# A batch of 64x64 matrix exponentials: from one 64-partition half to both halves of the partitions

## The chip, the cores and the metric

The kernel runs on one core of a Trainium2 chip. Time is device time in microseconds (us) of one execution of the program on that core. The core's engines work side by side and are ordered by semaphores: TensorE (PE, matrix products; its weight loads are listed as PEld), VectorE (DVE), ScalarE (ACT), GpSimd (POOL) and SyncE (SP, which here only issues DMAs). The profile is taken from one execution of its own. Its lines name the source line (L1355 is line 1355 of the kernel), the engine, and the tile written and those read.

## The reference

The input `x` has 4 batches of 512 tokens with 288 channels. A transformer block comes first, and then a rotation that depends on the batch:

```python
h = modulate(ln(x)); attn = 16 heads of width 18; x = x + g_msa * proj(attn)
xn = modulate(ln(x)); 4 experts, each token goes to 2 of them
x = x + g_mlp * moe(xn)

U, _ = qr(P)                                   # 288 x 64
v = silu(cond) @ W.T + b                       # 2016 numbers per batch
A = skew-symmetric 64 x 64 matrix made of v    # one per batch
R = expm(A)                                    # 64 x 64, one per batch
z = x @ U
x_out = x + (z @ R - z) @ U.T
```

Everything is float32. The change lies in the path from `v` to `U (R - I)`: four skew matrices of 64x64, one per batch, their exponentials, and the product with `U`.

## The kernel before

The whole work is in `fast_path`; a second path, `general_path`, runs only where a flag at the end says that some bound did not hold. All instructions are issued in an order written out by hand, so each engine takes its instructions in the order of the source as it is executed.

**Stage 1, attention** (about the first 336 us). A loop over `n`, 16 pairs of a batch and a group of four heads, and inside it over `t`, four blocks of 128 keys. Each of these 64 steps issues: `weigh` (four products `z` at L1676, in four groups of 32 rows of the array, and two exponentials `es` at L1685 on ACT), `gather` of the step before (four products `av` at L1694, in four groups of 32 columns), then the pieces that the dictionary `steps` has for this place (projections `pq` L1653, values `pv` L1623, transposes `pt` L1141, the merge `po` L1750, routing, and `column`, one step of a Householder factorisation of `P` on DVE, L1480 to L1523), then one piece from the list `beside`, then one or two `scatter_next`. The two `z` tiles are the only ones, so the `z` of a step waits until the exponentials of the step before have read theirs.

`beside` holds, among others, the two chains that the change touches. `skew_matrices` loads `W`, makes `v` on PE, stores it row by row into a 64x(4x64) matrix `udr` in DRAM (66 DMAs on SP, L1264) that POOL has cleared by a store of zeros (L1236), loads it back as `um` (L1271, SP), and subtracts the transpose: `A = um - um^T` (L1276, L1279). `rotations` returns the pieces of the exponential, and `exponentials` puts an empty piece behind each of them, so that one comes in every second step:

- `norm`: four copies of the identity `I4` (L1315), and a sum of squares per batch (`sqa`, L1321);
- `levels`: their sums over the partitions (`pf`, L1333), six comparisons that say how often each batch's matrix is to be halved (L1338 to L1345), the scaled matrix `pw[0]` (L1346) and its negative `An` (L1349);
- `power(1..3)`: the powers of the matrix, four products `pw` at L1355 and a copy (L1362) each;
- `horner(3..0)`: a polynomial of degree 16 in groups of four, with DVE operations on all four batches at once (L1374, L1376, L1380, L1384) and, but for the first, four products `ph` at L1355;
- `turn`: the transpose `Y` of the result `X` (`pxt`, L1389, and a copy, L1390);
- `square(0..5)`: eight products `psq` (L1395 and L1398: `X X` and its transpose) and two copies under a mask (L1402, L1403);
- `last`: `X - I` (L1406).

All of these tiles have 64 partitions, and 4x64 columns: the batches lie side by side. Every product therefore works with the rows 0 to 63 and the columns 0 to 63 of the array.

`bank` hands out PSUM tiles in turn from a few buffers, so that a product can wait for a copy that reads an earlier tile of another chain.

Routing: when the second batch of a half is merged, DVE computes the slots of its tokens (`slots_of`, L2003) and POOL then sends 16 scatters `slots<-xr` (L2006), one after the other. After them the rows of the first expert are loaded (`xg`, L2050 to L2055), and PE transposes these (`pt`, L2089) at the end of stage 1.

**Stage 2, the experts** (to about 712 us): eight expert passes, `hidden` (`ph`, L2295 and L2308) and `outputs` (`pe`, L2355), one piece of the list `rest` after each tile of work. Among these pieces are the rest of the factorisation, which gives `uT` (`U^T`, held twice, in partitions 0 to 63 and 64 to 127), then `all_fit` (the flag, with `norms`), and `subspace`: `UR = U^T` times `X`, three products `pu` (L2269), each followed by a copy (L2276). `finish` uses `UR` at L2421, `pz`.

**The end** (to 743.7 us): the last four pairs of token tiles are loaded, added, rotated and stored.

Of the kernel before, what the change touches and what calls it, by code (L numbers as in the profile page):

```python
# [10 lines left out]
F32 = mybir.dt.float32  # L11
# [7 lines left out]
P = 128  # L19
# [794 lines left out]
def fast_path(  # L814
# [60 lines left out]
    A = big.tile([D, B, D], F32, name="A")  # L875
# [6 lines left out]
    norms = big.tile([P, B + 1], F32, name="norms")  # L882
    XY = big.tile([D, 2, B, D], F32, name="XY")
# [70 lines left out]
    with ExitStack() as s1:  # L954
# [261 lines left out]
        def skew_matrices(between):  # L1216
# [6 lines left out]
            um = skew.tile([D, B, D], F32, name="um")  # L1223
# [5 lines left out]
            def loads():  # L1229
                for i in range(4):  # L1230
                    nc.gpsimd.dma_start(
                        out=wr[:, :, ts(i, width)],
                        in_=wrT[:, ts(i, width)].rearrange("(k p) f -> p k f", p=CC),
                    )
                nc.gpsimd.memset(um, 0.0)
                nc.gpsimd.dma_start(out=udr, in_=um)  # L1236
                nc.gpsimd.memset(brs, 0.0)
                for i in range(4):
                    nc.gpsimd.dma_start(
                        out=brs[i * HQ : i * HQ + B, :],  # L1240
                        in_=br[ts(i, width)].partition_broadcast(B),
                    )
# [27 lines left out]
            def load():  # L1270
                nc.sync.dma_start(out=um, in_=udr)  # L1271

            def last():
                pt = bank([P, N], "ptA")
                for b in range(B):
                    nc.tensor.transpose(  # L1276
                        pt[:D, ts(b, D)], um[:, b, :], ident[:D, :D]
                    )
# [3 lines left out]
                    pt[:D, : B * D],  # L1282
# [14 lines left out]
        def rotations():  # L1297
# [4 lines left out]
            fs = ep.tile([D, B], F32, name="fs")  # L1302
            need = ep.tile([D, SQUARINGS_FAST, B], F32, name="need")
            shrink = ep.tile([D, B], F32, name="shrink")
            I4 = ep.tile([D, B, D], F32, name="I4")
            pw = ep.tile([D, 4, B, D], F32, name="pw")
            An = ep.tile([D, B, D], F32, name="An")
# [6 lines left out]
            def norm():  # L1314
                nc.vector.tensor_copy(  # L1315
                    I4, ident[:D, :D].unsqueeze(1).to_broadcast([D, B, D])
                )

                for b in range(B):
                    sq = ep.tile([D, C], F32, tag="pr", name=f"sqa{b}")  # L1320
# [10 lines left out]
            def levels():  # L1331
                pf = bank([P, N], "pf")
                nc.tensor.matmul(pf[:D, :B], every[:D, :D], fs, start=True, stop=True)  # L1333
                nc.vector.tensor_copy(norms[:D, :B], pf[:D, :B])

                nc.vector.memset(shrink, 1.0)
                for k in range(SQUARINGS_FAST):
                    nc.vector.tensor_scalar(  # L1338
                        need[:, k, :], norms[:D, :B], THETA2 * 4.0**k, None, ALU.is_gt
                    )  # L1340
                    fk = ep.tile([D, B], F32, tag="fk", name=f"fk{k}")
# [5 lines left out]
                    pw[:, 0], A, shrink.unsqueeze(2).to_broadcast([D, B, D]), ALU.mult  # L1347
                )
                nc.vector.tensor_scalar_mul(An, pw[:, 0], -1.0)  # L1349

            def product(name, lhsT, rhs):
                pa = bank([P, N], name=name)
                pa = pa[:D, : B * D].rearrange("p (b d) -> p b d", b=B)
                for b in range(B):
                    nc.tensor.matmul(  # L1355
                        pa[:, b, :], lhsT[:, b, :], rhs[:, b, :], start=True, stop=True
                    )
# [8 lines left out]
            def horner(i):  # L1366
# [7 lines left out]
                nc.vector.tensor_scalar_mul(m, I4, c[0])  # L1374
# [11 lines left out]
            def turn():  # L1386
                pa = bank([P, N], "pxt")
                for b in range(B):
                    nc.tensor.transpose(pa[:D, ts(b, D)], X[:, b, :], ident[:D, :D])  # L1389
                nc.vector.tensor_copy(flat(Y), pa[:D, : B * D])  # L1390

            def square(k):
                pa = bank([D, 2, B, D], f"psq{k}")
                for b in range(B):
                    nc.tensor.matmul(  # L1395
                        pa[:, 0, b, :], Y[:, b, :], X[:, b, :], start=True, stop=True
                    )
                    nc.tensor.matmul(  # L1398
                        pa[:, 1, b, :], X[:, b, :], Y[:, b, :], start=True, stop=True
                    )  # L1400
                mask = need[:, k, :].bitcast(I32).unsqueeze(2).to_broadcast([D, B, D])
                nc.vector.copy_predicated(X, mask, pa[:, 0])  # L1402
                nc.vector.copy_predicated(Y, mask, pa[:, 1])  # L1403

            def last():
                nc.vector.tensor_sub(X, X, I4)  # L1406
# [11 lines left out]
        def triangular():  # L1418
# [160 lines left out]
            def half():  # L1579
# [4 lines left out]
                    norms[:D, B:], R, AX.X, ALU.max, apply_absolute_value=True  # L1584
                )
                nc.vector.tensor_scalar_mul(norms[:D, B:], norms[:D, B:], 64.0)
# [194 lines left out]
        BH = B // HALVES  # L1781
# [454 lines left out]
    with ExitStack() as s2:  # L2236
# [28 lines left out]
        def subspace():  # L2265

            for k in range(NK):
                pa = bank([P, N], f"pu{k}")
                nc.tensor.matmul(  # L2269
                    pa[:CC, : B * D],  # L2270
                    uT[:D, ts(k, CC)],
                    XY[:, 0].rearrange("p b d -> p (b d)"),
                    start=True,
                    stop=True,
                )
                nc.vector.tensor_copy(  # L2276
                    UR[:, k].rearrange("p b d -> p (b d)"), pa[:CC, : B * D]
# [179 lines left out]
        def all_fit():  # L2457
# [4 lines left out]
            for i, limit in enumerate((1.0e30, 1.0e20)):  # L2462
# [17 lines left out]
            small_ = fin.tile([P, B + 1], F32, name="small_")  # L2480
# [13 lines left out]
                float(P * (2 * B * NG + HALVES * E + B + 1)) - 0.5,  # L2494
# [138 lines left out]
```

## Time and profile before

| what | value |
|---|---|
| median of 3 runs | 745.1 us (744.53 to 746.78) |
| the profiled execution's own time | 745.39 us |
| its span | 743.7 us |
| PE busy | 705.4 us (95%) |
| DVE busy | 503.3 us (68%) |
| ACT busy | 279.9 us (38%) |
| POOL busy | 232.5 us (31%) |
| stretch 120 to 300 us: PE busy | 174.4 of 180 us |
| stretch 120 to 300 us: DVE busy | 144.9 of 180 us |
| products `pw`, `ph` at L1355 | 155.1 to 219.9 us, 48 matmul records |
| products `psq` at L1395 and L1398 | 236.5 to 292.8 us, 96 matmul records |

The span is the time from the first to the last instruction; 1.7 us of the execution lie outside it. A product in float32 appears as two matmul records and two weight loads; a transpose appears as one of each. A form such as `64*96 64x256` gives the rows and columns of the array that are used, and then the moving operand (partitions x columns). The views used below: the timeline of one engine (start, length, engine, line, operation, tiles, form, count, and in brackets the idle time before it with what ended it), the groups of instructions by form (busy time and mean duration in ns), and the chain that ended last, which follows the last instruction back through what released each one.

### The profile page before, as it was taken

What the parts mean: (1) busy time and instruction counts of PE and PEld (TensorE: products, weight loads), DVE (VectorE), ACT (ScalarE), POOL (GpSimd) and SP (SyncE); (2) the same over time, 40 slices, a digit from 0 to 9 for tenths busy, and PEclk for the clock granted to TensorE, in tenths of its full rate; (3) what the DMA queues carried; (4) which work ended last, traced back from release to release, by engine and by line L of the source; (5) the groups of instructions that cost most, each with busy time, mean ns of one, the idle gap of its engine ahead of it and who ended that gap; (6) DMA issues with size and microseconds to landing.
All of it is one profiled execution on the core that took longest, in us unless ns stands there. A gap on an engine that the chain in (4) does not pass through costs nothing.

```text
span 743.7 us, 11406 instructions
## 1 busy us (share of the span) xinstructions
PE 705.4 (95%) x3627; PEld 404.4 (54%) x3627; DVE 503.3 (68%) x2222; ACT 279.9 (38%) x431; POOL 232.5 (31%) x323
## 2 busy tenths in 40 slices
PE   5999999999999999989999999999999999999936
PEld 4432334334343435325677777777677676767723
DVE  3565778796987777885189888988888882013223
ACT  2455554454535444554223323232232323213202
POOL 4035900610035023750154253613123040232331
PEclk9999999999999999999999999999999999999977
DMA  9547700000000001055142543255353240342133
GB/s 227 144 127 205 258 3 6 1 2 2 2 1 2 3 26 59 34 152 136 57 119 66 177 116 121 77 138 168 66 167 72 84 143 18 96 153 73 48 110 128
DMA packets 65493, 66.68 MB, mean 90 GB/s; under 512 B 31608, under 2 KB 55965, under 8 KB 65424
## 3 DMA queue, kind: packets, MB, share of 16 engines
q1 hardware_dynamic: 57040, 41.90, 20.5%
q0 software_dynamic: 7360, 22.91, 9.5%
q10 hardware_dynamic: 1024, 1.07, 0.6%
q8 instruction: 30, 0.49, 0.3%
q14 instruction: 39, 0.32, 0.1%
HBM read 48.08 MB, written 18.09 MB: 89 GB/s over the span
## 4 chain that ended last, share of the span: by engine, by line
PE 67%; DVE 13%; DMA 6%; issue 6%; POOL 4%; ACT 2%; SPq 1%; DVEq 0%; POOLq 0%; ACTq 0%
PE pe L2355 19%; PE ph L2295 18%; PE pq L1653 6%; PE z L1676 4%; PE po L1750 4%; PE ph L2308 3%; PE av L1694 3%; PE pv L1623 2%; DMA rr<-den 2%; PE pt L2089 1%; DVE wj L1487 1%; ACT es L1685 1%; DMA yc<-chosen 1%; DVE q L1476 1%; DMA xg<-slots 1%
## 5 line engine op out<-in xcount | busy, mean ns | idle before, releaser
L2355 PE MATMUL pe<-w2s,hm 128*128 128x288 f32 (+1 forms) x648 | 164.2, 408 | 0.0
L1685 ACT ACTIVATE es<-z 128x1024 f32<-128x1024 f32 x128 | 124.1, 1021 | 83.8 <-PE z L1676 83.8
L2295 PE MATMUL ph<-xgT,w1s 128*128 128x288 f32 (+2 forms) x576 | 152.0, 413 | 0.4
L2355 PEld LDWEIGHTS pe<-w2s,hm 128*128 128x128 f32 (+1 forms) x648 | 118.4, 187 | 31.0 <-issue 2.1
L2295 PEld LDWEIGHTS ph<-xgT,w1s 128*128 128x128 f32 x576 | 105.7, 190 | 40.6 <-issue 11.3
L2317 ACT ACTIVATE hm<-ph,b1r 128x576 f32<-128x576 f32 (+2 forms) x72 | 49.8, 737 | 130.1 <-PE ph L2308 130.1
L1676 PE MATMUL z<-qk 32*128 32x512 f32 x512 | 89.9, 640 | 3.0 <-ACT es L1685 3.0
L1653 PE MATMUL pq<-hT,wqk 96*128 96x512 f32 x192 | 90.5, 608 | 0.0
L2367 POOL TENSOR_TENSOR y<-y,gb 128x288 f32<-128x288 f32 x36 | 29.7, 826 | 144.5 <-ACT y L2366 144.4
L1694 PE MATMUL av<-es,vt 128*32 128x512 f32 x512 | 68.8, 605 | 0.0
L1653 PEld LDWEIGHTS pq<-hT,wqk 96*128 96x128 f32 x192 | 34.3, 191 | 53.9 <-issue 39.2
L2366 ACT ACTIVATE y<-pe,weight 128x288 f32<-128x288 f32 x36 | 18.0, 500 | 118.3 <-PE pe L2355 118.3
L2006 POOL DMA_INDIRECT slots<-xr,where x32 | 32.7, 1021 | 92.4 <-DVE where L2003 48.6
L1676 PEld LDWEIGHTS z<-qk 32*128 32x128 f32 x512 | 25.8, 182 | 48.4 <-ACT es L1685 32.4
L1760 POOL TENSOR_TENSOR xs<-xs,og 128x288 f32<-128x288 f32 x16 | 12.6, 801 | 125.7 <-DVE og L1759 125.7
L1660 ACT ACTIVATE qk<-pq,bqk 128x512 f32<-128x512 f32 x32 | 22.0, 687 | 69.9 <-PE pq L1653 68.1
L1476 DVE SCALAR_TENSOR_TENSOR q<-q 64x1 f32<-64x1 f32 (+1 forms) x192 | 43.5, 226 | 7.0
L2368 POOL DMA_INDIRECT chosen<-y,place x36 | 36.8, 1021 | 19.2 <-DMA chosen<-y,place 10.3
L1487 DVE STREAM_SHUFFLE wj<-pt 32x288 f32<-32x288 f32 (+47 forms) x96 | 42.1, 438 | 0.7
L1694 PEld LDWEIGHTS av<-es,vt 128*32 128x32 f32 x512 | 10.2, 108 | 48.4 <-issue 42.6
L1750 PE MATMUL po<-wp,oT 128*128 128x288 f32 x128 | 33.8, 412 | 1.1 <-DVE oT L1734 0.6
L1475 DVE RECIPROCAL q<-q 64x1 f32<-64x1 f32 (+1 forms) x192 | 30.5, 159 | 4.4
(269 smaller groups left out, 911.6 us busy)
## 6 DMA issues: line engine op xcount, KB each, us to landing
w2s<-in_w_dram SPq DMA_DIRECT2D x8, 1296.0 KB
w1s<-in_w_dram SPq DMA_DIRECT2D x8, 1152.0 KB
slots<-empty POOLq DMA_DIRECT2D x36, 148.0 KB, 2.8
yc<-chosen SPq DMA_DIRECT2D x8, 576.0 KB
out_dram<-xs SPq DMA_DIRECT2D x8, 288.0 KB
wr<-in_wrT_dram POOLq DMA_DIRECT2D x4, 567.0 KB, 8.8
xg<-slots SPq DMA_DIRECT2D x4, 512.0 KB
xg<-slots SPq DMA_DIRECT2D x3, 640.0 KB
```

The source lines that it names most:

```text
L1476: nc.vector.scalar_tensor_tensor(s, u, part, s, ALU.mult, ALU.add)
L1487: nc.vector.stream_shuffle(wj[o : o + HQ, j:], pt[o0 : o0 + HQ, j:], [j % HQ] * HQ)
L1653: nc.tensor.matmul(pq, wqk[:, k, i, ts(g, P)], hT[:, k, :], start=(k == 0), stop=(k == NK - 1),)
L1676: nc.tensor.matmul(zs[c // 2][:, c % 2, :], qk[ts(c, HQ), 1, ts(t, P)], qk[ts(c, HQ), 0, :], start=True, stop=True,)
L1685: nc.scalar.activation(e, z, AF.Exp, scale=SCALE)
L1694: nc.tensor.matmul(avs[n][ts(c, HQ), :], vts[b % 2][:, t, 4 * g + c, :], es[c // 2][:, c % 2, :], start=(t == 0), stop=(t == NT - 1),)
L1750: nc.tensor.matmul(po, oTs[b][:, g, ts(t, P)], wp[:, g, :], start=(g == 0), stop=(g == NG - 1),)
L2006: nc.gpsimd.indirect_dma_start(out=slots[h], out_offset=bass.IndirectOffsetOnAxis(ap=where[:, i, t : t + 1], axis=0), in_=xrs[t // NT][:, ...
L2295: nc.tensor.matmul(ph[:, j, :SB], w1s[:, k, ts(f, P)], xgT[:, k, ts(j, SB)], start=(k == 0), stop=False,)
L2317: nc.scalar.activation(hm[:, f, : CAPS[r]].rearrange("p (j s) -> p j s", j=NB), ph[:, :, :SB], AF.Gelu_apprx_tanh, bias=b1r[:, h, r, f : f ...
L2355: nc.tensor.matmul(po[ts(m, rows), :], slots_[:, f, :], w[:, f, :], start=(f == 0), stop=(f == NF - 1),)
L2368: nc.gpsimd.indirect_dma_start(out=chosen[h], out_offset=bass.IndirectOffsetOnAxis(ap=place[:, t : t + 1], axis=0), in_=y, in_offset=None, ...
```

## The change

Two batches go to partitions 0 to 63 and two to partitions 64 to 127. The tiles `A`, `XY`, `um`, `fs`, `need`, `shrink`, `I2` (was `I4`), `pw`, `An` and `norms` have 128 partitions and half the columns. `each` issues the products of one batch of either half in turn: the products of the first half use the rows 0 to 63 and columns 0 to 63 of the array, those of the second the rows 64 to 127 and columns 64 to 127, and both write one PSUM tile, to partitions 0 to 63 and 64 to 127. The transposes at L1276 and L1389 become products with the identity. The last squaring no longer computes the transpose. The store of zeros and the load of `um` become two DMAs each, and `pf` two products. `subspace` makes two groups of three products, one for each half, with one copy for each group.

```diff
-    A = big.tile([D, B, D], F32, name="A")
+    BH = B // 2
+    A = big.tile([2 * D, BH, D], F32, name="A")
-    norms = big.tile([P, B + 1], F32, name="norms")
-    XY = big.tile([D, 2, B, D], F32, name="XY")
+    norms = big.tile([P, BH + 1], F32, name="norms")
+    XY = big.tile([2 * D, 2, BH, D], F32, name="XY")
...
-                nc.gpsimd.dma_start(out=udr, in_=um)
+                for h in range(2):
+                    nc.gpsimd.dma_start(
+                        out=udr[:, ts(h, BH), :], in_=um[ts(h, D), :, :]
+                    )
...
             def load():
-                nc.sync.dma_start(out=um, in_=udr)
+                for h in range(2):
+                    nc.sync.dma_start(out=um[ts(h, D), :, :], in_=udr[:, ts(h, BH), :])

             def last():
                 pt = bank([P, N], "ptA")
-                for b in range(B):
-                    nc.tensor.transpose(
-                        pt[:D, ts(b, D)], um[:, b, :], ident[:D, :D]
-                    )
+                for b in range(BH):
+                    for h in range(2):
+                        at = ts(h, D)
+                        nc.tensor.matmul(
+                            pt[at, ts(b, D)],
+                            um[at, b, :],
+                            ident[at, at],
+                            start=True,
+                            stop=True,
+                        )
...
             def norm():
-                nc.vector.tensor_copy(
-                    I4, ident[:D, :D].unsqueeze(1).to_broadcast([D, B, D])
-                )
-
-                for b in range(B):
-                    sq = ep.tile([D, C], F32, tag="pr", name=f"sqa{b}")
+                for h in range(2):
+                    at = ts(h, D)
+                    nc.vector.tensor_copy(
+                        I2[at], ident[at, at].unsqueeze(1).to_broadcast([D, BH, D])
+                    )
+
+                for b in range(BH):
+                    sq = ep.tile([P, C], F32, tag="pr", name=f"sqa{b}")
...
-                nc.tensor.matmul(pf[:D, :B], every[:D, :D], fs, start=True, stop=True)
-                nc.vector.tensor_copy(norms[:D, :B], pf[:D, :B])
+                for h in range(2):
+                    at = ts(h, D)
+                    nc.tensor.matmul(
+                        pf[at, :BH], every[at, at], fs[at, :], start=True, stop=True
+                    )
+                nc.vector.tensor_copy(norms[:, :BH], pf[:, :BH])
...
+            def each(out_, lhsT, rhs):
+
+                for b in range(BH):
+                    for h in range(2):
+                        at = ts(h, D)
+                        nc.tensor.matmul(
+                            out_[at, b, :],
+                            lhsT[at, b, :],
+                            rhs[at, b, :],
+                            start=True,
+                            stop=True,
+                        )

             def product(name, lhsT, rhs):
                 pa = bank([P, N], name=name)
-                pa = pa[:D, : B * D].rearrange("p (b d) -> p b d", b=B)
-                for b in range(B):
-                    nc.tensor.matmul(
-                        pa[:, b, :], lhsT[:, b, :], rhs[:, b, :], start=True, stop=True
-                    )
+                pa = pa[:, : BH * D].rearrange("p (b d) -> p b d", b=BH)
+                each(pa, lhsT, rhs)
                 return pa
...
             def turn():
-                pa = bank([P, N], "pxt")
-                for b in range(B):
-                    nc.tensor.transpose(pa[:D, ts(b, D)], X[:, b, :], ident[:D, :D])
-                nc.vector.tensor_copy(flat(Y), pa[:D, : B * D])
+                nc.vector.tensor_copy(Y, product("pxt", X, I2))

             def square(k):
-                pa = bank([D, 2, B, D], f"psq{k}")
-                for b in range(B):
-                    nc.tensor.matmul(
-                        pa[:, 0, b, :], Y[:, b, :], X[:, b, :], start=True, stop=True
-                    )
-                    nc.tensor.matmul(
-                        pa[:, 1, b, :], X[:, b, :], Y[:, b, :], start=True, stop=True
-                    )
-                mask = need[:, k, :].bitcast(I32).unsqueeze(2).to_broadcast([D, B, D])
+                pa = bank([P, 2, BH, D], f"psq{k}")
+                mask = need[:, k, :].bitcast(I32).unsqueeze(2).to_broadcast([P, BH, D])
+                each(pa[:, 0], Y, X)
+                more = k + 1 < SQUARINGS_FAST
+                if more:
+                    each(pa[:, 1], X, Y)
                 nc.vector.copy_predicated(X, mask, pa[:, 0])
-                nc.vector.copy_predicated(Y, mask, pa[:, 1])
+                if more:
+                    nc.vector.copy_predicated(Y, mask, pa[:, 1])
...
         def subspace():
-            for k in range(NK):
-                pa = bank([P, N], f"pu{k}")
-                nc.tensor.matmul(
-                    pa[:CC, : B * D],
-                    uT[:D, ts(k, CC)],
-                    XY[:, 0].rearrange("p b d -> p (b d)"),
-                    start=True,
-                    stop=True,
-                )
+            for h in range(2):
+                pa = bank([P, N], f"pu{h}")
+                pa = pa[:CC, : NK * BH * D].rearrange("p (k n) -> p k n", k=NK)
+                for k in range(NK):
+                    nc.tensor.matmul(
+                        pa[:, k, :],
+                        uT[ts(h, D), ts(k, CC)],
+                        XY[ts(h, D), 0].rearrange("p b d -> p (b d)"),
+                        start=True,
+                        stop=True,
+                    )
                 nc.vector.tensor_copy(
-                    UR[:, k].rearrange("p b d -> p (b d)"), pa[:CC, : B * D]
+                    UR[:, :, ts(h, BH), :].rearrange("p k b d -> p k (b d)"), pa
                 )
```

The remaining lines change the shapes of the small tiles in the same way, and the count that the flag is compared with.

## The prediction

> **What bounds the kernel now.** I read the page's shares first: PE is busy for 95% of the span. The chain that ended last agrees, with 67% PE and 13% DVE.
>
> ```profile
> PE 705.4 (95%) x3627; PEld 404.4 (54%) x3627; DVE 503.3 (68%) x2222; ACT 279.9 (38%) x431; POOL 232.5 (31%) x323
> ...
> PE 67%; DVE 13%; DMA 6%; issue 6%; POOL 4%; ACT 2%; SPq 1%; DVEq 0%; POOLq 0%; ACTq 0%
> ```
>
> What the change touches runs from 137 to 303 us and at 672 us, so the question is whether an instruction saved there moves what follows. PE's timeline of 136 to 345 us shows it:
>
> ```profile
> 155.08 0.68 PE L1355 MATMUL pw<-pw,An 64*64 64x64 f32 x8 [0.79 <-DVE An L1349]
> 155.68 1.14 PE L1676 MATMUL z<-qk 32*128 32x512 f32 x8
> ...
> 161.86 0.64 PE L1141 MATMUL pt<-ident,xh 128*96 128x128 f32 x4 [0.82 <-DVE pw L1362]
> ...
> 210.50 4.15 PE L1750 MATMUL po<-wp,oT 128*128 128x288 f32 x16 [0.51 <-DVE og L1759]
> ...
> 228.08 0.41 PE L1389 MATMUL pxt<-ident,XY 64*64 64x64 f32 x4
> 228.42 1.14 PE L1676 MATMUL z<-qk 32*128 32x512 f32 x8
> ...
> 236.47 0.33 PE L1395 MATMUL psq<-XY 64*64 64x64 f32 x2
> 236.63 0.28 PE L1398 MATMUL psq<-XY 64*64 64x64 f32 x2
> ...
> 237.54 1.14 PE L1676 MATMUL z<-qk 32*128 32x512 f32 x8
> ...
> 332.76 0.63 PE L2089 MATMUL pt<-ident,xg 128*128 128x128 f32 x4 [1.78 <-DMA xg<-slots]
> ```
>
> Read it thus: eight records of `pw` hold PE for 0.60 us before the next `z`, the sixteen of one squaring for 1.07 us, four transposes for 0.34 us. Few gaps lie between; the ones that matter are in brackets, and they name DVE three times and at the end a load. Where a `z` waits for ACT's exponential, that exponential followed the `z` before it, so an earlier start passes through.
>
> The last gap leads to POOL's timeline:
>
> ```profile
> 268.49 1.13 POOL L2006 DMA_INDIRECT slots<-xr,where  x1 [33.53 <-DVE where L2003]
> 271.90 0.98 POOL L2006 DMA_INDIRECT slots<-xr,where  x1 [2.28 <-DMA slots<-xr,where]
> ...
> 302.42 0.30 POOL L1120 TENSOR_SCALAR rs<-mv 128x4 f32<-128x4 f32 x1 [0.60 <-DVE mv L1119]
> ...
> 322.16 0.93 POOL L2050 DMA_DIRECT2D xg<-slots  x1 [2.12 <-DMA slots<-xr,where]
> ```
>
> The scatters start when DVE has `where` (268 us) and pace themselves by their landings, some 2.8 us each, up to the load that PE awaits at 332.76. From there to 712 us PE has no gap worth naming, so what is gained by 332 us is gained at the end.
>
> **PE's price of a product.** Squaring starts a record every 0.057 us (0.28 us for two, the next pair 0.117 us later). Do two quarters run side by side? Two kinds of half do: at `pz` (twelve records, two column halves) two start within 0.03 us, and `z` starts four row groups within 0.03 us.
>
> ```profile
> 685.32 0.88 PE L2421 MATMUL pz<-xT,UR 96*64 96x128 f32 x12
> ```
>
> The twelve records leave PE after 0.81 us. One behind the other, at 128/64 of 0.057 us, they would need 1.37 us. Quarters on the diagonal share neither rows nor columns; no row shows two row groups writing one PSUM tile at once. Bounds: full overlap (half the time) and none (0.057 us each as now), and below that a stop at every switch (rivals). I take full overlap, the nearest rows being `pz` and `z`. Then:
> - a product of four batches, 8 records in pairs, saves 4 x 0.057 = 0.23 us; there are six (`pw`, `ph`);
> - squarings 0 to 4, 16 records: 0.46 us each; the last keeps 8 of 16 records and pairs them: 12 x 0.057 = 0.69 us;
> - the transposes become 8 records, four pairs: about 0 (without overlap +0.23 us each);
> - `pf` has 4 records for 2, at most +0.15 us. PE waits there 0.92 us, until DVE's last `sqa` at 145.9 us; four `sqa` become two, so the cover stays.
>
> The Trainium skill speaks against this: "TensorEngine Tiling (Array Packing)", section "Restrictions and Gotchas", says that different row tiles write different PSUM banks and cannot access the same one simultaneously, and here both halves write one bank. By that rule the pairs take turns and the sum is the no-overlap one below; no run so far shows either.
>
> **DVE's price.** An operation goes by columns, not by partitions: `of` at L1953 with 128x256 takes 0.41 us, as the 64x256 ones at L1376 do. From the two rows below, a column costs (692 - 448) / 224 = 1.09 ns, so 128 fewer save 0.14 us; I take 0.13.
>
> ```profile
> L1734 DVE TENSOR_TENSOR oT<-oraw,rd 128x512 f32<-128x512 f32 x9 | 6.2, 692 | 0.8
> ...
> L1759 DVE TENSOR_TENSOR og<-po,gates 128x288 f32<-128x288 f32 x8 | 3.4, 448 | 4.5 <-PE po L1750 4.5
> ```
>
> Bounds are 0 and 0.2 us (the 64x64 `sqa` takes 0.21). The cheaper kind (L1349, L1374: 0.28 us, and 0.15 at 64x4) saves 0.07 us. The six rounds of small comparisons stay.
>
> **The sum, along the chain.** The chain's view passes between DVE and PE, so I follow the shift of whichever is later.
> 1. To 155 us: POOL's `xh` and `xr` (eight operations, 140.7 to 147.4 us) and DVE's `xh` lead, untouched. `I2` in two parts and `sqa` are under POOL's cover. `pw[0]` saves 0.13, `An` 0.07: shift -0.20.
> 2. 161.86: PE waits 0.82 us for DVE's copy of `pw`, another 0.13 there: -0.33. The first product's saving is lost in that wait.
> 3. `pw` 2 and 3 on PE: -0.79 at 176 us. DVE waits for PE at 181.6 (`vt`) and takes this on.
> 4. 187 to 210: DVE leads. Two `horner` pieces, 0.07 + 4 x 0.13 = 0.59 each: -1.97. PE has -0.79 and two `ph`, -1.25, plus the 0.51 it waits at 210.50: -1.76. The later one holds: -1.76.
> 5. The third `ph`: -1.99. The other DVE savings (two `horner`, `turn`, 11 masked copies for 12) lie beside PE.
> 6. `turn` 0; squarings 0 to 2: -3.37 at 259.7. DVE's `vt` waits for PE at 263.5, and `where` at 268 follows: POOL's scatters start 3.37 earlier.
> 7. Squarings 3 to 5: PE -4.98 at 293 us. POOL's waits of 0.60 at 302.42 and 0.76 at 305.89, for DVE, go; late next is the spacing of the scatter at 304 (2.8 us behind the one at 300.83). POOL: about -4.5 by 306, and so is the load. PE's wait at 332.76 grows by the other 0.5.
> 8. `subspace`: now 1.78 us on PE, in which its third product waits for a copy (0.31 us without a matmul). After: 12 records of 128 columns, 0.114 us each, 1.37 us and about 0.14 to empty: -0.3. The two copies (96x384, about 0.55 us each) end before `pz` at 685 us.
>
> Together -4.8 us: 745.39 - 4.8 = 740.6 against the profiled execution. The median lies 0.3 below it: **740.3 us**, -0.65%.
>
> **DMAs.** POOL issues a second store of zeros, 0.57 us at 57 us; behind it are `brs`, of which the fourth waits 1.48 us for another reason, and which are first read at 78 us. SP issues a second load of `um`, 0.50 us at 126.5; behind it are the four `den` DMAs, which end 2 us before DVE reads them at 134.67, and `um`'s reader is at 136.6. Both cost nothing; without that cover, 0.5 us each.
>
> **Rivals.** *No overlap on PE.* The rule above speaks for it, `pz` and `z` against. Then the chain is -0.33 at 176, -0.84 at 210.5 (the 0.51 of wait, DVE's saving being larger), +0.23 for `turn`, -0.61 at `where`, about -1.1 on POOL, -0.3 at `subspace`: -1.4, 743.7 us. No measurable change; 0.3%, 2.2 us, is what can be told.
>
> *Slower: every switch between halves empties the array.* A lone record lasts 0.218 us against a pitch of 0.057, so a switch costs at most 0.16. A four-batch product has four switches, +0.64 for six; a full squaring eight, +1.28 for five; the last +0.64 - 0.46; `turn` +0.87. Five of the products count: 3.2 + 6.4 + 0.2 + 0.9 = 10.7, less about 1.2 of DVE's and the other savings: +9.5, 754.6 us. With some 72 switches it decides from (1.2 + 2.2) / 72 = 0.05 us each. Against it: the changes of row group in `z` cost nothing that shows.
>
> *Only part arrives.* POOL stays at `where`'s shift and the scatters' spacing gives nothing back: -3.4 - 0.3, 741.4 us. Speaks for it: each scatter but two waits for the one before. On the other side, `sqa` and `I2` out of POOL's way, or full DVE savings of 0.2, could bring -6.5: 738.6.
>
> **How the numbers follow.** Full overlap, in whole or in part: 0.75, from 738.6 to 741.9. No overlap 0.14, around 743.7. A switch that costs: 0.08. The rest, 0.03, is spread. The range to 744.4 takes in most of no overlap and leaves out the slow end: 738.5 to 744.4. Faster by over 0.3% (under 742.9): 0.75 and little of no overlap, 0.76; within: 0.15; slower: 0.09.
>
> **What would show it.** In the changed profile `z` should follow 0.37 us after a `pw` starts (now 0.60) and 0.61 after a squaring (now 1.07); DVE's 128x128 operations should take about 0.28 us; the scatters should start near 265.1 us; `ph` should begin at 338.1 - 4.5 = 333.6. Wrong would be: 0.60 and 1.07 unchanged (no overlap), more (switches), or a gap before 332 that eats the gain.

## The result: the same time, and the profile after

The changed kernel took 747.43 us (median of 20 runs, 744.33 to 749.8), the kernel before, beside it on the same chip, 747.54 us (20 runs, 743.78 to 749.57). The ratio is 1.000, 95% interval 0.9987 to 1.0014: no difference that can be measured. The forecast was 740.3 us against 745.1 us, the median of the first three runs of the kernel before: a ratio of 0.9936. So the 0.65% did not arrive.

The page of the changed kernel hardly differs in its shares: PE lost 1.2 us of busy time, DVE 3.0 us, and the chain that ended last runs 68% through PE.

```profile
PE 704.2 (94%) x3635; PEld 401.7 (54%) x3635; DVE 500.3 (67%) x2217; ACT 280.3 (38%) x431; POOL 231.7 (31%) x324
...
PE 68%; DVE 13%; DMA 6%; issue 5%; POOL 3%; ACT 2%; SPq 1%; DVEq 0%; POOLq 0%; ACTq 0%
```

PE's timeline of the changed kernel, 136 to 345 us, answers to the one shown of before (start, length, engine, line, operation, tiles, form, count, and in brackets the idle time before it and what ended it):

```profile
156.07 0.45 PE L1375 MATMUL pw<-pw,An 64*64 64x64 f32 x8 [0.66 <-DVE An L1368]
156.45 1.14 PE L1700 MATMUL z<-qk 32*128 32x512 f32 x8
...
158.52 0.64 PE L1144 MATMUL pt<-ident,xh 128*96 128x128 f32 x4
162.72 1.09 PE L1144 MATMUL pt<-ident,xh 128*96 128x128 f32 x4 [3.56 <-DVE pw L1391]
163.74 2.09 PE L1700 MATMUL z<-qk 32*128 32x512 f32 x8
165.76 1.94 PE L1718 MATMUL av<-es,vt 128*32 128x512 f32 x8
...
170.27 0.45 PE L1375 MATMUL pw<-pw,An 64*64 64x64 f32 x8
...
240.89 0.68 PE L1375 MATMUL psq<-XY 64*64 64x64 f32 x16
241.50 1.14 PE L1700 MATMUL z<-qk 32*128 32x512 f32 x8
...
293.95 0.45 PE L1375 MATMUL psq<-XY 64*64 64x64 f32 x8
294.33 1.14 PE L1700 MATMUL z<-qk 32*128 32x512 f32 x8
...
334.85 0.63 PE L2112 MATMUL pt<-ident,xg 128*128 128x128 f32 x4 [2.44 <-DMA xg<-slots]
335.41 1.55 PE L1700 MATMUL z<-qk 32*128 32x512 f32 x8
...
341.19 4.04 PE L2320 MATMUL ph<-xgT,w1s 128*128 128x320 f32 x14
```

In the kernel before, the first two groups of transposes stood on PE's timeline in one row:

```profile
157.75 1.08 PE L1141 MATMUL pt<-ident,xh 128*96 128x128 f32 x8
```

Three things are to be seen. First, the products became as short as forecast: `z` follows `pw` after 0.38 us (0.60 before), a full squaring after 0.61 (1.07), the last squaring after 0.38 (1.07). Second, there is a gap that was not there: at 162.72 the second group of transposes `pt` waits 3.56 us for DVE's copy of `pw`. Before, both groups ran in one go at 157.75 us, and only the third waited, 0.82 us, at 161.86. Third, what follows the gap is slow: `z` takes 2.09 us (1.14 behind `pw`, and 1.28 in this place before), `av` 1.94 instead of 1.06. The same happens again, after a shorter wait, at 334.85.

The slowness is the clock. These are windows of the changed kernel (stretch, its length, then the busy time and number of instructions of PE, PEld, DVE, ACT and POOL; the number behind these five is the granted clock of PE, then come the share of the DMA engines and GB/s):

```profile
160.00:162.00 2.00, 0.00 (x0) 0.00 (x0) 2.00 (x11) 0.28 (x1) 0.00 (x0) 0.98 0.04 3
162.00:164.00 2.00, 1.28 (x8) 0.90 (x12) 1.63 (x8) 0.15 (x1) 0.00 (x0) 0.50 0.01 1
164.00:166.00 2.00, 2.00 (x12) 0.46 (x16) 1.76 (x9) 0.70 (x2) 0.00 (x0) 0.50 0.00 0
166.00:168.00 2.00, 2.00 (x10) 0.36 (x3) 0.60 (x5) 2.00 (x3) 0.00 (x0) 0.50 0.00 0
168.00:170.00 2.00, 2.00 (x10) 1.49 (x8) 0.00 (x0) 1.13 (x2) 0.00 (x0) 0.81 0.01 1
```

So from about 162 to 169 us PE ran at half its clock, 0.50 in three windows. In the kernel before, the granted clock was 1.00 in all of these stretches.

DVE's timelines, first of the changed kernel, then of the kernel before, show what PE waited for: the copy is in its old place, behind the sixteen operations `pl` of the routing, of which one starts every 0.38 us.

```profile
162.00 0.46 DVE L1840 SCALAR_TENSOR_TENSOR pl<-xr,wg 128x288 f32<-128x288 f32 x1
...
162.38 0.29 DVE L1391 COPY pw<-pw 128x128 f32<-128x128 f32 x1
```

```profile
161.39 0.41 DVE L1362 COPY pw<-pw 64x256 f32<-64x256 f32 x1
```

So the copy came no later than before, seen from the work around it (9.81 us behind the start of the projection `pq` ahead of it, 9.94 before); another group of transposes now waits for it. In the built programs' lists of semaphores that each instruction waits for, the second group of batch 2 (`k` = 1 in `modulate_T`) waited for ACT before and the third for DVE; now the second waits for DVE and the third for nothing new. In stage 1 the order and number of the calls of `bank` did not change. Every third call there gets a buffer of its own; the others draw on a pool with two buffers under one tag, and the source does not say which of the two a tile gets: that is settled when the program is built. In the changed program the second and the third group have exchanged their buffers, so that the second now takes the buffer that the first `pw` has just used. Two later pairs are exchanged as well, a `pv` with a `pq` and a `psq` with a `pt`.

The executions lie about 1 us apart before the change has an effect, so I compare positions from the start of the projection `pq` just ahead of the first `pw` (151.45 us before, 152.57 after). The second `pw` then comes 5.1 us later than before (17.70 against 12.60 us). From there the gain builds up as planned: the last squaring ends only 0.3 us later than before. Then comes the second fall of the clock, and `ph` begins 2.0 us later in this execution.

### The profile page after: what moved, and what is told of

Read it like the earlier page. It is cut to its first block, busy times and chain, and to the rows that moved or that the text cites. A ratio compares the mean times of both kernels' runs of the same rounds, so it can differ in the third digit from the quotient of the medians.

```text
span 747.4 us, 11416 instructions
## 1 busy us (share of the span) xinstructions
PE 704.2 (94%) x3635; PEld 401.7 (54%) x3635; DVE 500.3 (67%) x2217; ACT 280.3 (38%) x431; POOL 231.7 (31%) x324
## 3 DMA queue, kind: packets, MB, share of 16 engines
q10 hardware_dynamic: 1024, 1.07, 0.6%
## 4 chain that ended last, share of the span: by engine, by line
PE 68%; DVE 13%; DMA 6%; issue 5%; POOL 3%; ACT 2%; SPq 1%; DVEq 0%; POOLq 0%; ACTq 0%
PE pe L2380 19%; PE ph L2320 18%; PE pq L1677 6%; PE z L1700 6%; PE po L1774 4%; PE ph L2333 3%; PE av L1718 3%; PE pv L1647 2%; DMA rr<-den 2%; DMA yc<-chosen 2%; ACT es L1709 1%; PE pt L2112 1%; DVE wj L1511 1%; DVE q L1500 1%; DMA xg<-slots 1%
## 5 line engine op out<-in xcount | busy, mean ns | idle before, releaser
L1500 DVE SCALAR_TENSOR_TENSOR q<-q 64x1 f32<-64x1 f32 (+1 forms) x192 | 45.4, 236 | 6.9
L1482 DVE SCALAR_TENSOR_TENSOR pt<-wj,uf,pt 64x288 f32<-64x288 f32 (+62 forms) x63 | 32.6, 517 | 2.2
```

Source lines behind the costliest of these rows:

```text
L1482: nc.vector.scalar_tensor_tensor(m, w, u[rows, :], m, ALU.mult, ALU.add)
L1500: nc.vector.scalar_tensor_tensor(s, u, part, s, ALU.mult, ALU.add)
```

## The experiments

The theory (A): every saving is made, and is lost again in one wait and in the slow clock behind it, which come from the exchange of two PSUM buffers. The rival (B): what was saved does not lie on the path that sets the end, and the wait only stands where other waits would stand.

**Buffers strictly in turn, in both kernels.** The same edit was made to the changed kernel (`after_rr`) and to the kernel before (`before_rr`): two tags of one buffer each, taken alternately.

```diff
-        return ps_m.tile(shape, F32, tag="m", name=name)
+        turns_m[0] += 1
+        tag = f"m{turns_m[0] % 2}"
+        return ps_m.tile(shape, F32, tag=tag, name=name, bufs=1)
+    turns_m = [0]
```

> The changed kernel, with one thing undone: `bank` takes its two main PSUM buffers strictly in turn, by two tags, where before the buffer was left to the allocator. By the instruction order the second transpose group `pt021` then waits for ACT's `qk`, as in the kernel before, and not for DVE's copy of the first power. Theory A (the gain was made and then lost in that one wait): the 3.56 us of PE idle at 159 us and the stretch at half clock behind it vanish, `pw` to `z` stays 0.38 us and squaring to `z` 0.61 us, the time is 3 to 5 us below before (ratio 0.993 to 0.996). The wait for `xg` at the end of stage 1 stays at 2 to 2.5 us. Theory B (the stage is paced by something else than PE and DVE, and what is saved turns into waits anyway): ratio 0.9985 to 1.0015, other waits grow in its place.

> The kernel before with the same strict turn of the two PSUM buffers and nothing else. Its waits in stage 1 are those of the kernel before; in stage 2 a few small products (`pR`) wait for PE where they waited for DVE. Both theories: ratio 0.9985 to 1.0015. If it is not the same, the turn itself costs or saves something and the run of the changed kernel has to be read against this one.

Measured: `after_rr` 744.08 us against 748.23 of the kernel before, ratio 0.9940 (0.9919 to 0.9961): faster. `before_rr` 747.38 us, ratio 0.9982 (0.9969 to 0.9995). So the turn itself gives the kernel before some 0.2%, a little more than expected; in its built program it changes no buffer of stage 1, only some in stage 2. With the turn on both sides the two programs have the same buffers throughout stage 1, and the change gives 0.9940 / 0.9982 = 0.9958, worked out, give or take about 0.0025. PE's timeline of `after_rr` in the place of the wait:

```profile
157.96 1.08 PE L1147 MATMUL pt<-ident,xh 128*96 128x128 f32 x8
...
162.16 0.64 PE L1147 MATMUL pt<-ident,xh 128*96 128x128 f32 x4 [0.92 <-DVE pw L1394]
...
164.35 0.45 PE L1378 MATMUL pw<-pw,An 64*64 64x64 f32 x8
```

Both first groups run in one go, as in the kernel before, the third waits 0.92 us, and the clock stays up. The second `pw` stands 12.34 us behind its `pq`, where the changed kernel had 17.70. The two other exchanged pairs left no trace in the time: the changed kernel is 5.4 us behind `after_rr` at the second `pw` and still 5.3 us at the end of the last squaring.

**The exchange alone, in the kernel before.** `before_swap` is `before_rr` with the two buffers of these groups exchanged, and nothing of the change.

```diff
+        swap = name in ("pt021", "pt022")
-        tag = f"m{turns_m[0] % 2}"
+        tag = f"m{(turns_m[0] + swap) % 2}"
```

> The kernel before with the strict turn, and the buffers of two transpose groups (`pt021` and `pt022`) exchanged, so that the second group waits for DVE's copy of the first power behind 32 routing operations, as in the changed kernel. No arithmetic is changed. Theory A: PE idles some 3 us near 159 us, PE's clock falls behind it, and the time rises by 4 to 6 us (ratio 1.005 to 1.008). Theory B: at most 1 us, ratio under 1.0015.

Measured: 752.98 us, ratio 1.0063 (1.0043 to 1.0082), which is 5.6 us over `before_rr`. PE's timeline of `before_swap`:

```profile
158.42 0.64 PE L1145 MATMUL pt<-ident,xh 128*96 128x128 f32 x4
162.52 1.09 PE L1145 MATMUL pt<-ident,xh 128*96 128x128 f32 x4 [3.46 <-DVE pw L1366]
163.53 2.09 PE L1680 MATMUL z<-qk 32*128 32x512 f32 x8
```

The same wait (3.46 us) and the same slow `z` appear without a single short product. Theory A stands: the exchange alone costs 5.6 us, at least as much as the change gains. B falls, because a gain arrives as soon as the exchange is undone.

**How much of the loss is wait, how much is clock.** `after_fill` is the changed kernel with its exchanged buffers; six products that nobody reads are put into the wait, in rows of the PSUM tile that the transposes leave free.

```diff
+            if (which, b, k) == (0, 2, 1):
+                for _ in range(6):
+                    nc.tensor.matmul(
+                        spare[0][CC:, :C], ident[:, CC:], xh[:, 0, :],
+                        start=True, stop=True,
+                    )
             pt = bank([P, N], f"pt{which}{b}{k}")
+            spare[0] = pt
```

> The changed kernel with its own choice of buffers, and six products of 288 columns that nobody reads put into PE's long wait at the second transpose group (into rows 96 to 127 of the PSUM tile just written). The wait's end, DVE's copy near 162.7 us, stays. If the lost time is wait and low clock, and the clock falls because PE idles: the clock stays at 1.00 behind it, z takes 1.14 us instead of 2.09 and av 1.06 instead of 1.94, pw2 starts near 168.2 instead of 170.27, and the execution is 1.5 to 2 us shorter, a ratio near 0.9975 where the changed kernel has 1.000. If the clock falls for another reason: z stays at 2.09 and the ratio at 1.000. If the products come in PE's way: above 1.000.

Measured: 745.98 us, ratio 0.9977 (0.9959 to 0.9995). PE's timeline of `after_fill`:

```profile
160.33 3.10 PE L1146 MATMUL pt<-xh,ident 128*32 128x288 f32 x12 [1.18 <-ACT hT L1156]
163.36 0.64 PE L1153 MATMUL pt<-ident,xh 128*96 128x128 f32 x4
163.94 1.14 PE L1709 MATMUL z<-qk 32*128 32x512 f32 x8
165.01 1.07 PE L1727 MATMUL av<-es,vt 128*32 128x512 f32 x8
```

The clock stays at 1.00, `z` takes 1.14 us and `av` 1.07. The added products even end late: the second group starts 0.61 us later, seen from `pq` (10.76 against 10.15 us), and the second `pw` all the same 1.31 us earlier (16.39 against 17.70). So by these two executions the slow clock cost 1.31 + 0.61 = 1.9 us. The second `pw` of the undisturbed order stands at 12.32 us, so the whole loss was 5.4 us, and the other 3.5 us are the wait. So work that nobody reads brought forward what follows it. Of this, 1.28 us were still there at the end of the last squaring, and none at `ph` (188.84 us behind `pq`, 188.62 in the changed kernel): this execution waited 0.42 and 2.06 us for `xg`, and there its clock fell too. The ratio lies below the 1.000 of the changed kernel, but the two intervals overlap, so a gain in the whole time is not shown.

**The second wait.** At the end of stage 1 PE waits for the last columns of `xg`. In its profiled execution `after_rr` waited 0.44 and 2.32 us, with a fall of the clock behind it (0.54 and 0.61 in the windows 329 to 331 and 331 to 333 us). The same kernel was run again (`after_rr_again`), and twenty transposes of the identity were put into this wait (`after_rr_fill`).

```diff
-                pt = bank([P, NK, P], f"pt{i}{t}")
+                pt = bank([P, NK + 1, P], f"pt{i}{t}")
                 for k in range(NK):
+                    if (i, t, k) == (0, 0, 2):
+                        for _ in range(20):
+                            nc.tensor.transpose(pt[:, NK, :], ident, ident)
                     nc.tensor.transpose(pt[:, k, :], xg[:, t, ts(k, P)], ident)
+                pt = pt[:, :NK, :]
```

> The changed kernel with its PSUM buffers strictly in turn, once more, beside the other kernels of this group. Every theory: a ratio of about 0.994 to the kernel before, PE's wait at the third transpose group near 0.9 us, PE's wait for xg 2.3 us with a lower granted clock for some 5 us behind it.

> Buffers in turn, and twenty transposes of the identity that nobody reads put into PE's wait for the last columns of xg at the end of stage 1. They end at about the time at which the load lands, so the third transpose of the tile stays near 329.3 us. If the fall of the clock behind that wait costs time of its own: z takes about 1.1 to 1.4 us instead of 2.09, ph begins 1.0 to 1.4 us earlier (about 334.3 instead of 335.57), and the ratio falls from 0.994 to about 0.9925. If PE is held by ACT's exponentials there anyway: ph begins at the same time and the ratio stays 0.994.

Measured: `after_rr_again` 742.43 us against 747.29, ratio 0.9948 (0.9930 to 0.9966); `after_rr_fill` 742.24 us, ratio 0.9940 (0.9922 to 0.9959). PE's timelines, first of `after_rr`, then of `after_rr_again`, then of `after_rr_fill`:

```profile
329.34 1.08 PE L2115 MATMUL pt<-ident,xg 128*128 128x128 f32 x4 [2.32 <-DMA xg<-slots]
330.35 2.09 PE L1703 MATMUL z<-qk 32*128 32x512 f32 x8
...
335.57 4.58 PE L2323 MATMUL ph<-xgT,w1s 128*128 128x320 f32 x16
```

```profile
327.52 0.63 PE L2115 MATMUL pt<-ident,xg 128*128 128x128 f32 x4 [1.48 <-DMA xg<-slots]
328.08 1.14 PE L1703 MATMUL z<-qk 32*128 32x512 f32 x8
...
332.29 4.58 PE L2323 MATMUL ph<-xgT,w1s 128*128 128x320 f32 x16
```

```profile
328.30 2.35 PE L2117 MATMUL pt<-ident 128*128 128x128 f32 x20
330.49 0.61 PE L2118 MATMUL pt<-ident,xg 128*128 128x128 f32 x4
331.03 1.14 PE L1703 MATMUL z<-qk 32*128 32x512 f32 x8
...
335.24 4.57 PE L2327 MATMUL ph<-xgT,w1s 128*128 128x320 f32 x16
```

From the third transpose of the tile to `ph` it takes 6.23 us with the fall of the clock, 4.77 without it, and 4.75 with the wait filled: in these executions the fall cost 1.46 us. (Where the clock stayed low for longer, in `after_fill`, the same stretch took 7.73 us.) In the second execution of the same kernel the wait was 1.48 us, and the clock stayed up with nothing filled in, so that it was the filling that kept it up in `after_rr_fill` is not shown. The expected step to 0.9925 was not reached, and the two ratios can't be told apart: the fall comes in some executions only, so that filling the wait can save only a part of 1.46 us on average. In the profiles it came in this place in five of the seven of the changed kernel and its variants with the wait left as it is, and in none of the three of the kernel before and its variants.

**PE's share of the gain.** In `after_rr_twice` every product of the chain is issued twice. PE then has about its old price, while DVE's tiles stay short.

```diff
-                for b in range(BH):
-                    for h in range(2):
+                for b, h in [(b, h) for b in range(BH) for h in range(2)] * 2:
+                    if True:
```

> Buffers in turn, and every product of the chain is issued twice (the second writes the same numbers again). On PE this gives back what the quarters save: 16 paired records should take 0.61 us where 8 took 0.38, which is the 0.60 us of the kernel before, and a full squaring 32 records, near 1.07 us; the transpose gets 0.27 us longer than before and the last squaring stays 0.46 us shorter. DVE's shorter tiles and the shorter subspace stay. If PE's price carries the gain, as the prediction's chain has it, the ratio goes from 0.994 to about 0.998. If DVE's tiles carry it: the ratio stays near 0.995.

Measured: 744.81 us against 747.12, ratio 0.9968 (0.9951 to 0.9985). PE's timeline of `after_rr_twice`:

```profile
237.55 1.15 PE L1378 MATMUL psq<-XY 64*64 64x64 f32 x32
238.63 1.14 PE L1703 MATMUL z<-qk 32*128 32x512 f32 x8
```

A squaring of 32 records has PE's old price again, 1.08 us (and a product of 16 has 0.61). The ratio lies between the two expectations. The interval holds 0.998 and only just leaves out 0.995, and it overlaps that of `after_rr_again`. So by the times it is not shown how much the shorter products carry. The positions in the traces say more. Behind `pq`, the last squaring ends at 141.44 us in `before_rr`, at 140.24 in `after_rr_twice` and at 136.40 in `after_rr_again`: 3.8 of the 5.0 us go when the products have their old price. At the load of `xg` it is 3.3 of 5.2 us (170.65, 168.72 and 165.43). The rest is there without the shorter products, with DVE's shorter operations; how it is split more finely stays open, as doubling does not restore every old price (the transpose is longer, the last squaring shorter).

**Do the pairs have to stand next to each other?** The changed code issues one product of each half in turn. `after_rr_seq` issues the two of the first half, then the two of the second; `after_rr_seq8` does so over a whole squaring, four products of the first half and then four of the second.

```diff
-                for b in range(BH):
-                    for h in range(2):
+                for h in range(2):
+                    for b in range(BH):
```

```diff
+            def half(h, out_, lhsT, rhs):
+                at = ts(h, D)
+                for b in range(BH):
+                    nc.tensor.matmul(
+                        out_[at, b, :],
+                        lhsT[at, b, :],
+                        rhs[at, b, :],
+                        start=True,
+                        stop=True,
+                    )
...
-                each(pa[:, 0], Y, X)
                 more = k + 1 < SQUARINGS_FAST
-                if more:
-                    each(pa[:, 1], X, Y)
+                for h in range(2):
+                    half(h, pa[:, 0], Y, X)
+                    if more:
+                        half(h, pa[:, 1], X, Y)
```

> Buffers in turn, and the products of all batches of the first half are issued before those of the second, so that neighbours in the queue no longer lie in different quarters; the instructions and DVE's tiles stay the same. If the gain comes from two quarters working side by side: z follows a pw after 0.60 us (0.38 in pairs) and a squaring after 1.07 us (0.61), and of the 4 us of gain about 3 go: the prediction's sum without overlap is -1.4 us, a ratio near 0.998. If PE's price is that of fewer or shorter instructions, or the gain comes from DVE's shorter tiles: 0.38 and 0.61 us stay and so does the ratio, 0.994.

> Buffers in turn, and in a squaring all eight records of the first half are issued ahead of the eight of the second (four and four twice, in the run in which the first half came first). If PE lets records of another quarter begin though many of the first quarter stand ahead of them in its queue: z still follows a squaring after about 0.66 us. If it looks only a few records ahead: between 0.75 and 1.0 us. If the two halves never ran side by side and the records are shorter for another reason: 0.66 us too, but the records then start one at a time, 0.03 us apart, and not two at a time.

Measured: `after_rr_seq` 741.63 us, ratio 0.9933 (0.9912 to 0.9953), as fast as the pairs; a single run of `after_rr_seq8` took 745.62 us. PE's timeline, first of `after_rr_seq`, then of `after_rr_seq8`:

```profile
256.82 0.73 PE L1378 MATMUL psq<-XY 64*64 64x64 f32 x16
257.48 1.14 PE L1703 MATMUL z<-qk 32*128 32x512 f32 x8
```

```profile
258.31 0.96 PE L1389 MATMUL psq<-XY 64*64 64x64 f32 x16
259.20 1.14 PE L1715 MATMUL z<-qk 32*128 32x512 f32 x8
```

0.66 us in the first, 0.89 in the second, 0.61 in pairs and 1.07 before. Short windows count the records of a squaring that are under way (stretch, its length, PE's busy time with the number of records, granted clock, DMA share, GB/s); first `after_rr_seq`, 0.17 us from its start, then `after_rr_seq8`, at the same distance:

```profile
256.99:257.01 0.02, 0.02 (x6) 1.00 0.00 0
```

```profile
258.48:258.50 0.02, 0.02 (x3) 1.00 0.00 0
```

Six records against three; at this distance the kernel before has three too, and the pairs of `after_rr_again` six. So I was wrong in the expectation for the first: with two products of one half ahead of two of the other, twice as many records are still under way. With four ahead they go one behind the other at first, and of the 0.46 us saved 0.28 are lost. That excludes the reading that the records are simply shorter, since the order alone changes the price of the same sixteen. I read it so that the halves run side by side, and that PE reaches a few records ahead for it: two products are within that reach and four are not. That is argued and not shown, as the trace does not say which quarter each record used.

## Why the prediction was wrong, step by step

The table follows the prediction's own chain. Each position is taken from the start of the `pq` ahead of the first `pw`; the second column is `after_rr_again` less `before_rr` (both with buffers in turn), the third the changed kernel less the kernel before, from the profiles named.

| place (us in the profile before) | forecast | buffers in turn | as changed |
|---|---|---|---|
| 1: first `pw` (155) | -0.20 | -0.15 | -0.13 |
| 2: third `pt` group (162), second `pw` behind it in the last column | -0.33 | -0.28 | +5.10 |
| 3: third `pw` done (176) | -0.79 | -0.72 | +4.65 |
| 4: `po` (210.5) | -1.76 | -1.85 | +3.49 |
| 5: third `ph` done (220) | -1.99 | -2.08 | +3.27 |
| 6: squaring 2 done (260) | -3.37 | -3.42 | +1.93 |
| 6: first scatter (268.5) | -3.37 | -3.42 | +1.91 |
| 7: last squaring done (293) | -4.98 | -5.04 | +0.31 |
| 7: load of `xg` issued (322) | -4.5 | -5.22 | +0.54 |
| 7: `ph` of the first expert (338) | -4.5 | -5.39 | +1.96 |

**Step 2 failed.** It reads: PE waits 0.82 us at 161.86 for DVE's copy of `pw`, "another 0.13 there". It took for granted that the wait stays with the third group of transposes. In the changed program the second group waited in its place, 3.56 us, with a slow clock behind it, and the second `pw` came 5.1 us later where 0.33 earlier was forecast. Which buffer a tile of `bank` gets was treated as a property of the source, and it is one of the built program. No term of the sum and no rival asked what it would cost if the second group, which runs some 3.5 us earlier, had the buffer of `pw`. The profile of before had the number: the copy starts at 161.39 us behind the routing, and the second group ran at 158.3, so some 3 us lay open. The closing sentence on "a gap before 332 that eats the gain" named the sign to look for, but neither place nor price. That the result came out at 1.000 is chance: the gain and the loss only happen to be of one size.

**What held.** With the buffers in turn, steps 1 to 6 came out within 0.1 us each: the mechanism of the gain was right. The prices under them: a product 0.22 us shorter (forecast 0.23), a squaring 0.46 (0.46), the last one 0.69 (0.69), `turn` 0.04 longer (about 0), DVE's copy 0.29 us (about 0.28), `An` 0.23 us (0.28 less 0.07).

**Where sizes were off.** The load of `xg` came 5.2 us earlier in this pair of executions, and 4.7 in `after_rr`, the same kernel, where 4.5 was forecast: single landings of the scatters differ from execution to execution (one wait was 2.12 us in `after_rr_again` and 2.72 in `after_rr`, beside 3.37 in `before_rr`). The wait for `xg`, expected to grow by 0.5 us from 1.78 us, was 2.44 in the changed kernel, 0.44 + 2.32 in `after_rr` and 1.48 in `after_rr_again`. That a longer wait there can also cost a fall of the clock, 1.46 us, was not in the sum. The last row of the table is the good case: in `after_rr`, with the fall, `ph` came only 2.6 us earlier than in `before_rr`. `subspace` saved 0.65 us and not 0.3, as PE's timeline of the changed kernel shows; its two groups no longer wait for a copy:

```profile
674.87 1.19 PE L2294 MATMUL pu<-XY,uT 64*96 64x128 f32 x12
676.00 3.72 PE L2320 MATMUL ph<-xgT,w1s 128*128 128x256 f32 x16
```

**The rivals.** No overlap on PE and a costly switch are both excluded by 0.38 and 0.61 us. That only part arrives by way of POOL is excluded too: the load of `xg` came earlier by more than `where` did. The quoted rule of the Trainium skill, "TensorEngine Tiling (Array Packing)", "Restrictions and Gotchas", that different row tiles cannot access one PSUM bank at the same time, does not show here: two quarters on the diagonal wrote one tile, in different partitions, at 0.61 us for sixteen records where one behind the other took 1.07. (The prediction's remark that no row shows two row groups writing one tile at once goes too far: in `weigh` each `z` tile takes the products of two row groups, into different halves of its columns.)

As a version of its own, the changed kernel with buffers in turn (`after_rr`) is faster than the kernel before: 0.9940 and 0.9948 in two groups of runs, with `after_rr_seq` at 0.9933 not to be told from it. By the ratios that is 3.9 to 4.5 us, some 0.2% of which is the turn itself. The change alone, with the turn on both sides, gives about 3.1 us (0.9958), give or take some 1.9 us; the forecast of 4.8 us lies within that.

## What to carry to other kernels

When a change alters the length or shape of work that shares rotating buffers with other chains, ask for each neighbour what it would wait for if it got another buffer, and price that from the place of the releasing instruction in its engine's queue; where the pool leaves the choice open, fix the turn by hand before judging the change. A wait of PE that grows by a few microseconds can have a second price, the slower clock behind it. And a change with no net effect may hold a gain and a loss of the same size: compare positions from a common instruction along the timeline, and see where they jump.

## What the runs showed of the hardware

**The clock falls for a fixed time, and not by the length of the wait alone.** PE's granted clock fell to about 0.50 with waits of 3.56 us (162 us in the changed kernel), 3.46 (`before_swap`), 2.44 (335 us in the changed kernel), 0.44 and 2.32 (`after_rr`), 0.44 and 2.15 (`after_rr_seq8`), 0.42 and 2.06 (`after_fill`) and 1.77 us (`after_rr_seq`). It stayed at 1.00 behind 1.92 (the second wait of `before_swap`), 1.82 (`before_rr`), 1.78 (before) and 1.48 us (`after_rr_again`). PE's timeline of `after_rr_seq` shows the shortest wait with a fall:

```profile
329.03 0.63 PE L2115 MATMUL pt<-ident,xg 128*128 128x128 f32 x4 [1.77 <-DMA xg<-slots]
```

From the windows' mean clocks, counting what is missing to 1.00 as time at 0.50, I estimate each slow stretch at 3.4 us (335 us in the changed kernel, `before_swap`, `after_rr`, `after_rr_seq`, `after_rr_seq8`) or at twice that, 6.8 us (`after_fill`, and 162 us in the changed kernel: 0.08 + 6.0 + 0.76). At 335 us it even began after PE had resumed: the window 333 to 335 us has 1.00, 335 to 337 has 0.75, and PE resumed at 334.85. The Trainium skill, "TensorE: Matmul & The Clock Gate", Part 1, describes a gate with two states that judges activity in free-running windows of about 3.4 us. The two states, the lengths of 3.4 and 6.8 us and the late fall agree with that. It puts the fall after an idle window of about 3.4 us; here a wait of 1.77 us was enough once, so the measurement decides: shorter waits can do it, and not each time. One reading is left open. At the end of stage 1 only transposes stand on either side of the wait. Counted from the end of the last `av` before it to the first `z` behind it, the time was 3.4 to 4.2 us in four of the falls and 2.70 in that of `after_rr_seq`, and the clock stayed up at 2.71 (before), 2.75 (`before_rr`), 2.86 (`before_swap`), and with the transposes filled in at 2.94 (`after_rr_fill`). Whether transposes count as work for the clock no run here separates.

**Products in quarters on the diagonal overlap, also when they are not neighbours in the queue.** Two products of one half ahead of two of the other cost 0.66 us for sixteen records, against 0.61 in strict alternation and 1.07 in one quarter; four ahead cost 0.89 (one profile).

**Executions of one kernel differ by several microseconds.** 743.8 to 749.6 us before and 744.3 to 749.8 after; a small gain has to be read from ratios over many runs, and its place from positions inside the traces.
